# Routing of the last entry pair at the end of attention: one entry moved between the halves of the other's output projection, the rest alternated with early expert tiles

## The chip, the cores and the metric

The kernel runs on one NeuronCore of a Trainium2 chip. The metric is the device time of one execution in microseconds (us). Engines are named as in the profile: PE (TensorE matmuls), PEld (its weight loads), DVE (VectorE), ACT (ScalarE), POOL (GpSimd) and SP (SyncE, which here only issues DMAs).

## What is computed

All data are float32. An input of 2 x 2048 tokens of width 256 passes through four residual blocks: a state-space block, an expert layer, an attention block, and the same expert layer once more.

```python
x = x + attn_a(layernorm(x), ...)     # state-space scan
x = x + ffn(layernorm(x), Wr, br, Wl1, bl1, Wl2, bl2, biases_N)
x = x + attn_b(layernorm(x), w_qkv, w_out, ln_w, ln_b)   # attention over the 2 entries
x = x + ffn(layernorm(x), Wr, br, Wl1, bl1, Wl2, bl2, biases_N)
```

In the expert layer a router scores 8 experts for each token, the best two are kept, and their normalised weights mix the two results; an expert is `(silu(x W1a + b1a) * (x W1b + b1b)) W2 + b2` with a hidden width of 512. The attention here mixes only the two batch entries of one position with each other, in 16 heads of 64.

## The kernel before

**Groups.** Tokens are worked in groups of 512: four groups in time, `s` = 0 to 3 (`NS` = 4), for each of two batch entries `i` = 0, 1. Below, (0,3) is the first entry of the last group and (1,3) the second.

**Attention.** For each `s`, the loop at the end runs `mix(s)` (L1431: value projections times attention weights into two tiles `o`), `outward(s)` (L1454: the output projection), and then half of the scores of the next `s`. `outward` runs over the two entries and, in each, over two halves of two token tiles; a half is 16 matmuls into `pao` (L1462, each shown as two records), an addition to the residual `x` on DVE (L1470), and `aside.step(2)` (L1471).

**Work at the side.** `aside` is a list of Python generators. `aside.step(n)` runs the first one on to its n-th next `yield`, going over to the next generator when one ends; `aside.rest()` runs all of them to the end. So each `step` writes a piece of other work into the program at that point. After each entry `outward` appends `prepared(i, s)`, which routes that entry, and for the last group also `entered()`, which writes the routed entry's rows into the expert table.

**Routing of one entry**, `prepare` (L309), has six yields: (1) the write of `x` to the output (L316, SP) and the layernorm statistics; (2) the inverse root on POOL (L244); (3) the normalised `xn` (L248, DVE) and its write to `xnd` in DRAM (L318, SP); (4) eight transposes `pt_g` (L257), two ACT copies, eight router matmuls `pr_g` (L330); (5) the choice of two experts on DVE (L338 to L357); (6) two prefix matmuls `pk_g` (L363, L364) and the places `at` (L391); then the weights `pay` (L396 to L410), with one exponential on ACT (L398).

**Entering** (L412) then issues eight indirect DMAs from POOL (L433), each of which writes 128 rows of 12 bytes into the table, with a yield after every second one.

**Early tiles.** An expert tile is 256 token slots of one expert. Nine of them (called tiles 0 to 8 here; `ge` in names) are planned before routing is complete and are worked inside attention by the generator `last.early`, held in `tiles`. One tile takes three steps. The first fetches the weights of the next tile (L668 and L670, 1 MB and 0.5 MB, and the biases L672, L674, all on SP) with its two gathers (L683, POOL), transposes its own rows (`pxs`, L709, copied by ACT at L713), and does two of four up-projection parts (`pab`, L722; SiLU on ACT at L730, product on DVE at L731). The second does the other two parts. The third is the down-projection (`pf`, L792), the result `y` on DVE (L805), and two indirect DMAs that add the rows to the output (L816, POOL). Weights, gathered rows and `y` have two buffers each: tile n+2 loads its first weights when tile n's up-projection is over, and its second weights when its down-projection is.

**The end of attention.** At `s` = 3 `aside.rest()` empties the side list and `tiles.step(4)` brings the early tiles to the end of tile 1's up-projection. Then come `mix(3)` and `outward(3)`. Before the change, four steps of (0,3)'s routing were taken by the two `aside.step(2)` of the second entry; all that was left, and the whole of (1,3), was taken by `aside.rest()`; `last.plan()` (L515) plans the remaining tiles from the counts of all tokens on DVE; and `tiles.rest()` writes the rest of the early tiles, from tile 1's down-projection to tile 8. After that `last.run()` works the remaining tiles.

**What sets the order.** The order on SP is that of the program text. On the other engines a list scheduler orders the instructions inside this part; each engine then runs its own list strictly in order. Dependences through DRAM are tracked by tensor: the write of a whole entry of `x` to the output (L316) and the adding DMAs of early tiles (L816) stand in program order to each other, while the adding DMAs among themselves are declared independent.

Of the kernel before, what the change touches and what calls it, by code (L numbers as in the profile page):

```python
# [19 lines left out]
NS = L // TG  # L20
# [26 lines left out]
def kernel(  # L47
# [35 lines left out]
    def bank(tag, name):  # L83
        return ps.tile([P, 512], F32, tag=tag, name=name)
# [140 lines left out]
    aside = Aside()  # L225
# [672 lines left out]
    with tc.tile_pool(name="ssm1", bufs=1) as s1, tc.tile_pool(name="ssm2", bufs=2) as s2:  # L898
# [295 lines left out]
        tiles = Aside()  # L1194
# [65 lines left out]
    with tc.tile_pool(name="att1", bufs=1) as a1, tc.tile_pool(name="att2", bufs=2) as a2:  # L1260
# [33 lines left out]
        def prepared(b, s):  # L1294
            routed.append((order.index((b, s)) + 1, (yield from last.prepare(b, s, "T"))))

        def entered():
            while routed:
                n, group = routed.pop(0)
                yield from last.enter(*group)  # L1300
                if n in EARLY:
                    last.plan_early(n, EARLY[n], group[2])
                    tiles.step()
# [151 lines left out]
        def outward(s):  # L1455
            o = mixing[s]
            for i in range(2):
                for t in range(0, GT, 2):
                    po = bank("C", f"pao_{s}{i}{t}")
                    for j in range(2):  # L1460
                        for c in range(NA):
                            nc.tensor.matmul(  # L1462
                                po[:, j * DM : (j + 1) * DM],
                                o[i][:, c, (t + j) * P : (t + j + 1) * P],
                                w_o_sb[:, c, :],
                                start=(c == 0),
                                stop=(c == NA - 1),
                            )
                    x = xg[i, s][:, t : t + 2, :]
                    nc.vector.tensor_tensor(x, po.rearrange("p (t d) -> p t d", t=2), x, ALU.add)  # L1470
                    aside.step(2)  # L1471
                aside.add(prepared(i, s))
                if s == NS - 1 or s == NS - 2 and i:
                    aside.add(entered())
            if s + 3 < NS:
                aside.add(front(s + 3))
# [5 lines left out]
        tiles = Aside()  # L1482
# [5 lines left out]
        for s in range(NS):  # L1488

            if s + 1 < NS:  # L1490
                while s + 1 not in inputs:
                    aside.step()
                aside.add(entered())
                scores(s + 1, range(0, GT // 2))
            else:
                aside.rest()
                tiles.step(4)
            mix(s)
            outward(s)
            if s + 1 < NS:  # L1500
                scores(s + 1, range(GT // 2, GT))
                weights(s + 1)
        aside.rest()
        last.plan()
        tiles.rest()

# [63 lines left out]
```

## Time and profile before

| what | value |
|---|---|
| median of 3 runs | 1734.07 us (1732.85 to 1741.57) |
| profiled execution | 1733.28 us, of which 1731.6 us span |
| PE busy | 1596.9 us, 92% of the span |
| DVE, ACT, POOL busy | 901.2, 674.1, 734.1 us |
| mean granted TensorE clock | 0.969 |
| end of the last output projection | 1330.7 us from the span's start |
| early tiles 2 and 3: down-projection over | 1358.7 and 1380.5 us |
| one early tile after that | 11.8 us |
| last early tile (8): down-projection over | 1441.1 us |

A row of the timeline has the start, the busy time, the engine, line and operation, the tile written and those read, how many instructions are merged, and in brackets how long the engine was idle before it and what ended that. All times are us from the start of the span. In the list of waits, a row names the waiting engine and line, what it waited for, the time in total, how often, and the longest. "Remote" there means that the semaphore that was waited for came at no event that the profile can name.

### The profile page before, as it was taken

What the parts mean: (1) busy time and instruction counts of PE and PEld (TensorE: products, weight loads), DVE (VectorE), ACT (ScalarE), POOL (GpSimd) and SP (SyncE); (2) the same over time, 40 slices, a digit from 0 to 9 for tenths busy, and PEclk for the clock granted to TensorE, in tenths of its full rate; (3) what the DMA queues carried; (4) which work ended last, traced back from release to release, by engine and by line L of the source; (5) the groups of instructions that cost most, each with busy time, mean ns of one, the idle gap of its engine ahead of it and who ended that gap; (6) DMA issues with size and microseconds to landing.
All of it is one profiled execution on the core that took longest, in us unless ns stands there. A gap on an engine that the chain in (4) does not pass through costs nothing.

```text
span 1731.6 us, 21826 instructions
## 1 busy us (share of the span) xinstructions
PE 1596.9 (92%) x6928; PEld 1182.5 (68%) x6928; DVE 901.2 (52%) x2481; ACT 674.1 (39%) x1348; POOL 734.1 (42%) x702
## 2 busy tenths in 40 slices
PE   6997888989989997999998999899999699999997
PEld 4565555766767775787885575465768588888886
DVE  6778888737557465222237648447554522222222
ACT  4886877856546542222332202001121222333332
POOL 3346456445536565444442003403241543545443
PEclk9998998999989998999999999999999899999999
DMA  4111211634435362789852312606463568888882
GB/s 154 44 69 36 86 62 44 217 99 134 120 65 173 89 176 80 205 255 313 221 114 79 81 42 63 86 14 135 140 124 105 126 184 246 223 230 223 229 212 45
DMA packets 174742, 231.27 MB, mean 134 GB/s; under 512 B 45920, under 2 KB 138080, under 8 KB 174368
## 3 DMA queue, kind: packets, MB, share of 16 engines
q1 hardware_dynamic: 143520, 193.42, 37.8%
q0 software_dynamic: 31104, 36.42, 11.7%
q8 instruction: 56, 0.92, 0.2%
q14 instruction: 62, 0.51, 0.1%
HBM read 192.72 MB, written 37.06 MB: 133 GB/s over the span
## 4 chain that ended last, share of the span: by engine, by line
PE 66%; DMA 11%; DVE 11%; POOL 4%; ACT 3%; issue 3%; another core or an unknown queue 1%; SPq 0%; DVEq 0%; POOLq 0%; ACTq 0%
PE pab_g L722 8%; PE pao L1462 6%; PE pab_fe L722 5%; PE pq L1368 5%; PE pab_f L722 4%; PE pf_g L792 4%; PE pab_ge L722 4%; PE pf_fe L792 3%; PE pvd L1442 3%; DVE xc L1047 3%; PE pk L1368 3%; PE pf_f L792 2%; DMA lb<-sums 2%; PE pi L1143 2%; PE pc L1030 2%
## 5 line engine op out<-in xcount | busy, mean ns | idle before, releaser
L722 PE MATMUL pab_fe<-xT_fe,w_fe 128*128 128x256 f32 x672 | 163.1, 399 | 25.0 <-DVE gT_fe L731 18.5
L722 PEld LDWEIGHTS pab_fe<-xT_fe,w_fe 128*128 128x128 f32 x672 | 132.4, 200 | 53.8 <-DVE gT_fe L731 23.2
L722 PE MATMUL pab_g<-xT_g,w_g 128*128 128x256 f32 x736 | 162.9, 379 | 0.0
L722 PEld LDWEIGHTS pab_g<-xT_g,w_g 128*128 128x128 f32 x736 | 139.4, 190 | 19.1 <-ACT xT_g L713 0.4
L816 POOL DMA_INDIRECT out_dram<-y_g,tab_g x51 | 80.3, 1574 | 141.4 <-DVE y_g L805 62.0
L1368 PE MATMUL pq<-w_qkv_sb,axT 128*128 128x512 f32 x256 | 117.4, 598 | 0.0
L1047 DVE SCALAR_TENSOR_TENSOR xc<-pre,conv_w_sb,xc 128x512 f32<-128x512 f32 x144 | 112.5, 791 | 6.2 <-ACT xc L1039 5.5
L1462 PE MATMUL pao<-w_o_sb,o 128*128 128x256 f32 x512 | 112.0, 380 | 1.3 <-DVE o L1450 1.2
L1462 PEld LDWEIGHTS pao<-w_o_sb,o 128*128 128x128 f32 x512 | 97.0, 190 | 18.1 <-issue 2.9
L731 DVE SCALAR_TENSOR_TENSOR gT_g<-pab_g,b_g,sa_g 128x256 f32<-128x256 f32 x92 | 44.5, 484 | 117.8 <-ACT sa_g L730 107.8
L730 ACT ACTIVATE sa_g<-pab_g,b_g 128x256 f32<-128x256 f32 x92 | 43.6, 474 | 154.4 <-PE pab_g L722 140.9
L433 POOL DMA_INDIRECT table_g<-pay_g,at_g x64 | 62.1, 970 | 88.4 <-DVE w_g L409 55.0
L1030 PE MATMUL pc<-xT,w_in_sb 128*128 128x512 f32 x192 | 94.8, 623 | 0.4 <-ACT xc L1039 0.4
L792 PE MATMUL pf_g<-w_g,gT_g 128*128 128x256 f32 x408 | 92.9, 379 | 0.0
L1084 ACT ACTIVATE lt<-lb,cum 128x128 f32<-128x128 f32 x256 | 82.8, 393 | 21.2 <-DMA lb<-sums 21.2
L731 DVE SCALAR_TENSOR_TENSOR gT_fe<-pab_fe,b_fe,sa_fe 128x256 f32<-128x256 f32 x84 | 39.7, 481 | 95.1 <-ACT sa_fe L730 87.3
L1368 PEld LDWEIGHTS pq<-w_qkv_sb,axT 128*128 128x128 f32 x256 | 48.8, 193 | 58.8 <-issue 57.2
L722 PE MATMUL pab_ge<-xT_ge,w_ge 128*128 128x256 f32 x288 | 68.6, 393 | 17.2 <-ACT xT_ge L713 12.1
L816 POOL DMA_INDIRECT resid<-y_fe,tab_fe x42 | 67.1, 1598 | 35.6 <-DVE y_fe L805 15.2
L792 PE MATMUL pf_fe<-w_fe,gT_fe 128*128 128x256 f32 x336 | 80.6, 394 | 1.4 <-DVE gT_fe L731 1.2
L792 PEld LDWEIGHTS pf_g<-w_g,gT_g 128*128 128x128 f32 x408 | 75.4, 190 | 9.3 <-DVE gT_g L731 0.2
L1383 ACT ACTIVATE kd<-pk 128x512 f32<-128x512 f32 x32 | 19.1, 597 | 158.3 <-PE pk L1368 88.1
(493 smaller groups left out, 3458.5 us busy)
## 6 DMA issues: line engine op xcount, KB each, us to landing
w_g<-in_wl_dram SPq DMA_DIRECT2D x28, 1024.0 KB
w_fe<-in_wl_dram SPq DMA_DIRECT2D x21, 1024.0 KB
lb<-sums SPq DMA_DIRECT2D x32, 512.0 KB
w_f<-in_wl_dram SPq DMA_DIRECT2D x16, 1024.0 KB
o<-prob SPq DMA_DIRECT2D x32, 512.0 KB
w_g<-in_wl_dram SPq DMA_DIRECT2D x28, 512.0 KB
w_fe<-in_wl_dram SPq DMA_DIRECT2D x21, 512.0 KB
w_ge<-in_wl_dram SPq DMA_DIRECT2D x9, 1024.0 KB
```

The costliest lines, as they stand in the source:

```text
L433: i = nc.gpsimd.indirect_dma_start(out=self.table, out_offset=bass.IndirectOffsetOnAxis(ap=at[:, t, c : c + 1], axis=0), in_=pay[:, t, c, ...
L722: nc.tensor.matmul(p[:, q * n : (q + 1) * n], t["w1"][:, k, c * P : (c + 1) * P], t["xT"][:, k, :], start=(k == 0), stop=(k == KD - 1),)
L730: nc.scalar.activation(sa[:, :n], p[:, 0:n], AF.Silu, bias=t["b1"][:, i : i + 1])
L731: nc.vector.scalar_tensor_tensor(t["gT"][:, i, :n], p[:, n : 2 * n], t["b1"][:, NHT + i : NHT + i + 1], sa[:, :n], ALU.add, ALU.mult)
L792: nc.tensor.matmul(pos[h][:, h * DM : (h + 1) * DM], t["gT"][:, j, h * P : (h + 1) * P], t["w2"][:, j, :], start=(j == 0), stop=(j == NHT ...
L816: j = nc.gpsimd.indirect_dma_start(out=self.acc if self.direct else self.acc[: self.seq[i][4] or NT + TT, :], out_offset=bass.IndirectOffs ...
L1030: nc.tensor.matmul(pc, w_in_sb[:, k, DI + c * P : DI + (c + 1) * P], xT[:, k, :], start=(k == 0), stop=(k == KD - 1),)
L1047: nc.vector.scalar_tensor_tensor(xc[:, c, :], pre[:, c, j : j + TG], conv_w_sb[:, c, j : j + 1], xc[:, c, :], ALU.mult, ALU.add,)
L1084: nc.scalar.activation(lt[:, i, :], lb[:, i, :], AF.Relu, bias=g["cum"][:, t, i : i + 1], scale=-1.0)
L1368: nc.tensor.matmul(p, src[:, k, t * P : (t + 1) * P], w_qkv_sb[:, k, j, half * TG : (half + 1) * TG], start=(k == 0), stop=(k == KD - 1),)
L1442: nc.tensor.matmul(pvd, w_qkv_sb[:, k, 2, c * P : (c + 1) * P], xd[:, k, :], start=(k == 0), stop=(k == KD - 1),)
L1462: nc.tensor.matmul(po[:, j * DM : (j + 1) * DM], o[i][:, c, (t + j) * P : (t + j + 1) * P], w_o_sb[:, c, :], start=(c == 0), stop=(c == NA ...
```

## The change

Two edits. In `outward`, for the last group, each half is followed by four steps of the side list in place of two. At entry 0 the list is empty, so this acts on entry 1 alone: (0,3) is now taken eight steps, four between the halves and four behind them, which is its whole routing and half of its entering. And `aside.rest()` at the end becomes a loop that alternates one step of the side list with one step of the early tiles. In the program this moves (0,3)'s transposes and router matmuls on PE ahead of the last half of `pao`, and the early tiles' steps, with their weight loads on SP and their gathers and adding DMAs on POOL, in among the steps of (1,3). Nothing is added or removed.

```diff
                     x = xg[i, s][:, t : t + 2, :]
                     nc.vector.tensor_tensor(x, po.rearrange("p (t d) -> p t d", t=2), x, ALU.add)
-                    aside.step(2)
+
+                    aside.step(4 if s == NS - 1 else 2)
                 aside.add(prepared(i, s))
                 if s == NS - 1 or s == NS - 2 and i:
                     aside.add(entered())
...
             if s + 1 < NS:
                 scores(s + 1, range(GT // 2, GT))
                 weights(s + 1)
-        aside.rest()
+        while aside.waiting:
+            aside.step()
+            tiles.step()
         last.plan()
         tiles.rest()
```

The orders that result, as the two built programs have them (tile numbers as above):

| engine | before | after |
|---|---|---|
| PE | last half of pao; pt (0,3); pr (0,3) among pf of tile 1; pxs 2; pk (0,3), pt, pr and pk (1,3) among pab 2; pf 2; pxs 3 | pt (0,3); last half of pao with pr (0,3) in it; pk (0,3); pf 1; pxs 2; pt (1,3) and pab 2; pf 2; pxs 3; pr (1,3); half of pab 3; pk (1,3); rest of pab 3; pf 3 |
| POOL | half of gather 4; adds of tile 1; half of gather 4; 8 + 8 table writes; gather 5 and adds of tile 2 | half of gather 4; 6 table writes; adds of tile 1; 2 table writes; half of gather 4; gather 5 and adds of tile 2; 8 table writes |
| SP | x, xn (0,3); x, xn (1,3); weights 3; weights 4 | x, xn (0,3); weights 3; x, xn (1,3); weights 4 |

On SP, the write of x (1,3) waited in the program before only for its data and its queue; in the changed program it also waits for the two adds of tile 1, and the adds of tile 2 on POOL wait for it.

## The prediction

> **What bounds the kernel now.** I read the page's slices first: PE is busy in nine tenths or more of almost every slice, and the change touches the one late hole, slice 32 of 40 (1342 to 1385 us).
>
> ```profile
> PE   6997888989989997999998999899999699999997
> ```
>
> From 1450 to 1700 us PE is without a gap, so what is saved in the hole comes off the end. The timeline of PE there:
>
> ```profile
> 1346.46 1.56 PE L722 MATMUL pab_ge<-xT_ge,w_ge 128*128 128x256 f32 x6 [0.78 <-DVE gT_ge L731]
> ...
> 1349.82 1.99 PE L722 MATMUL pab_ge<-xT_ge,w_ge 128*128 128x256 f32 x8 [0.92 <-issue]
> ...
> 1356.41 2.43 PE L792 MATMUL pf_ge<-w_ge,gT_ge 128*128 128x256 f32 x10 [3.13 <-DVE cump_g L548]
> 1358.67 0.60 PE L709 MATMUL pxs_ge<-ident,xs_ge 128*128 128x128 f32 x4
> 1367.77 9.41 PE L722 MATMUL pab_ge<-xT_ge,w_ge 128*128 128x256 f32 x32 [8.51 <-ACT xT_ge L713]
> 1377.02 3.67 PE L792 MATMUL pf_ge<-w_ge,gT_ge 128*128 128x256 f32 x16
> ```
>
> The idle times in brackets, with one of 0.92 at 1338.40, sum to 14.3 us, and tile 3's 32 records take 9.41 us where tile 4's take 7.17. What is late? The last gap waits for ACT's copy of transposes that PE shows as over at 1359.3. The list of waits from 1335 to 1370:
>
> ```profile
> ACT xT_ge L713 <- remote: 12.4, 1, 12.4
> ...
> ACT sa_ge L730 <- remote: 4.9, 1, 4.9
> ```
>
> ACT waits 8 us after the work it needs; SP's second weights and POOL's next gather wait for PE's semaphore as well, and small DVE operations of the plan wait 1 to 2 us for one another. The semaphores lag on every engine. What runs meanwhile is on POOL:
>
> ```profile
> 1344.25 0.99 POOL L433 DMA_INDIRECT table_g<-pay_g,at_g  x1 [0.30 <-issue]
> ...
> 1363.23 0.95 POOL L433 DMA_INDIRECT table_g<-pay_g,at_g  x1 [0.30 <-issue]
> 1367.37 0.99 POOL L683 DMA_INDIRECT xs_ge<-xnd_g,tab_ge  x1 [3.19 <-remote]
> ```
>
> Sixteen table writes of 128 rows of 12 bytes, one each 1.26 us; the lag begins some 5 us into them and ends 3 us behind them. It is no accident of this place: semaphore events lag by up to 7.7 and 8.6 us in the sixteens from 1107 and from 1249, and at 667 to 690, where six writes, a pause of 7 us and eight writes stand in the first expert layer, PE shows
>
> ```profile
> 687.89 0.60 PE L709 MATMUL pxs_fe<-ident,xs_fe 128*128 128x128 f32 x4
> 692.03 8.86 PE L722 MATMUL pab_fe<-xT_fe,w_fe 128*128 128x256 f32 x32 [3.54 <-issue]
> ```
>
> nothing at the six, then 3.54 us idle at the eight. That the writes cause the lag is inferred from their standing together.
>
> **The change, part by part.** No instruction is added or taken out.
>
> *(0,3) between the halves.* The last half of pao is 32 records of 0.219 us, 7.0 us. Before it PE now does eight transposes (0.87 us) and in it the router matmuls (1.7 us), which until now stood behind it; pao ends at 1330.7 + 0.87 + 1.7 = 1333.3. On PE that is a trade at nothing: xn (0,3) is ready at 1321.6 (its DVE row ends then), the transposes come at 1323.7, and the pao matmul between covers ACT's copies of 0.6 us each; without that cover it would be 0.6 us. (1,3)'s residual is 2.6 us later. DVE then does (0,3)'s places among (1,3)'s statistics, and of pay's last steps one stands behind tile 1's second y, so pay is ready at about 1339.9, against 1342.2 before.
>
> *(1,3) and the early tiles.* PE: pk to 1333.8, tile 1's pf (3.5) to 1337.3, pxs 2 (0.45) to 1337.8. Then come six of eight transposes of (1,3), whose xn waits for statistics, POOL's power (1.04) and three DVE passes of 0.41: 1338.9, so PE waits about 1 us. Tile 2's pab 7.0 and the rest of the transposes: 1346.9; pf 2 to 1350.4; pxs 3, pr (1,3) 1.7: 1352.6; half of pab 3: 1356.1. There pk waits for DVE's choice, and tile 3's first SiLU stands on ACT behind (1,3)'s exponential and two table loads of 1.28 us; the product behind pk on DVE feeds the next PSUM bank. I take 1.5 us (ends: 0.8, the like gap at 1346.46, and 3). PE is at 1358, with pab 3 at 1361.5, with pf 3 at 1365.0. Before, tile 3's pf ends at 1380.5; from there a tile takes 11.8 us on both sides. Lead without any lag: 15.5 us.
>
> *The table writes.* They are no longer sixteen in a row: six from 1339.9, two adds of tile 1, two more to about 1354, then gathers and tile 2's adds, then (1,3)'s eight from about 1361 or a little later. What the lag costs then, no row shows for this order. Lower end: nothing, as at the six from 667. Upper end: the old price, 14.3 + 2.2. A pair of eights from 1183 and 1200 shows lags of 3.3 and 7.5 us (there PE had other work). I take the row at 692, for it is nearest: six, a break, eight, with an early tile's chain to be fed. Its price is 3.54 + (8.86 - 7.17) = 5.2 us; with 1 us for the first eight, 6.2.
>
> [...] I keep 6.2, since the row's 3.54 us gap did pay 1.69.
>
> *SP.* Tile 3's weights now go ahead of x and xn of (1,3). Their second half must wait for pf 1 (1337.3), as before (1338.4): free. But x (1,3) now waits for tile 1's adds, which POOL issues behind six table writes: 1339.9 + 6 x 1.26 = 1347.5, the second at 1349.4. [...] The trace's landing events of such adds are 3.6 to 4.6 us when DMA is calm and 6.6 under load; I take 5: 1354.4. Behind it on SP stand xn (1,3) and tile 4's weights, issued 1.8 us later, 1356.2; these landed 5.3 us after issue with one 0.5 MB write ahead of them, now there are two (1.4 more): 1363. [...] Xn (1,3) itself is read only by gathers of the last stage, about 1410. Tile 2's adds wait for x (1,3) on POOL to about 1358, and gather 5's second half behind them has until 1377. The plan on DVE ends before 1380, and SP needs it at about 1403.
>
> Sum: 15.5 - 6.2 = 9.3 us off the profiled execution's 1733.3: 1724.0. The median of the runs is 0.8 us above that execution: 1725.
>
> **Rivals.** *The pair of eights sets the price.* Lags of 3.3 and 7.5 us, less about 1 us of slack each, and 2.2 for the clock: 11, gain 4.5, 1730. For it: eight writes follow eight after about 8 us here too. Against: scatters and gathers stand between.
> *No lag at all*: eights are short enough. Gain 15.5, 1718.5. For it the six at 667; against it every eight in the trace.
> *The change doesn't do what it says*: the eights lag as the sixteen did, and the gap only moves. 15.5 - 14.3 - 0.5: 1733.
> *Slower.* The wait of x (1,3) on SP for tile 1's adds holds up tile 4's weights. Every us that the adds land after 1358 is a us of PE at tile 4; the lead is used up at 1358 + 9 = 1367, and half a per cent is lost at 1376, 27 us after issue. The longest landing of an indirect DMA in this part is 10 us, behind a queue of broadcasts, so it needs the writes of the table to dam the queue far more than they now do. 1744 then.
>
> **How the numbers follow.** A measurement of this kernel can tell about 0.5% from no change: 8.7 us, so faster means below 1725.4. Nearest row 45% (1725, half of it on either side of that bound), pair of eights 25% (1730), no lag 15% (1718.5), gap only moved 8% (1733), slower 7% (1744). Faster: 0.24 + 0.15 and a part of the spread of the pair, 0.46; slower 0.07; the rest 0.47. The range 1716 to 1733 takes in the first four but for their edges: the unknown costs are the lag (0 to 15 us) and the wait at pk (0.8 to 3).
>
> **What would show it.** Right: pao ends near 1333; tile 3's pf ends 8 to 14 us before 1380.5; the table writes stand as 6, 2 and 8; PE's gaps at tiles 2 and 3 are 1 to 2 us, with one of 3 to 5 at tile 4 or 5, by the end of the last eight, and a granted clock under 1 behind it. Wrong: gaps of over 5 us near 1350 or 1372; a wait of tile 4's pab for w_ge; gather 5 or 6 as what ends a PE gap; or tile 3 early but the last stage starting late, so that the lead is lost behind tile 8.

## The result, and the profile after

The changed kernel takes 1727.33 us, the median of 20 runs (1719.77 to 1738.76); the kernel before, run beside it, 1734.6 us (1728.1 to 1743.5, 20 runs). The ratio is 0.9962 with a 95% interval of 0.9948 to 0.9977, that is 6.6 us less (4.0 to 9.0). Forecast were 9.3 us less and 1725.0. The profiled execution of the changed kernel has a span of 1726.6 us, 5.0 less than that of before.

PE in the 40 slices of the page, after the change:

```profile
PE   6997888989989996999998999899999799999997
```

Slice 32 (1338 to 1381 us) is now at 7 in place of 6. The hole is shallower, but it is there. PE's timeline through it:

```profile
1324.52 6.29 PE L1462 MATMUL pao<-w_o_sb,o 128*128 128x256 f32 x28
...
1356.13 5.27 PE L722 MATMUL pab_ge<-xT_ge,w_ge 128*128 128x256 f32 x16 [1.39 <-DVE gT_ge L731]
1361.23 3.67 PE L792 MATMUL pf_ge<-w_ge,gT_ge 128*128 128x256 f32 x16
1364.74 0.60 PE L709 MATMUL pxs_ge<-ident,xs_ge 128*128 128x128 f32 x4
1367.83 3.72 PE L722 MATMUL pab_ge<-xT_ge,w_ge 128*128 128x256 f32 x16 [2.49 <-issue]
1377.50 6.51 PE L722 MATMUL pab_ge<-xT_ge,w_ge 128*128 128x256 f32 x16 [5.95 <-DVE gT_ge L731]
1383.85 3.67 PE L792 MATMUL pf_ge<-w_ge,gT_ge 128*128 128x256 f32 x16
1387.36 0.60 PE L709 MATMUL pxs_ge<-ident,xs_ge 128*128 128x128 f32 x4
```

Tile 3's down-projection is over at 1364.7, where the kernel before has 1380.5. But the one long gap has become one of 5.95 us in tile 4, with a slow clock behind it (granted 0.56; 16 records in 6.51 us where 3.72 is usual). Tile 4 ends at 1387.4 against 1392.3, and from there both kernels take 11.8 us a tile. On POOL, the table writes stand as forecast, six, two and eight. Shown are the last of the six, the adds behind them, and the first and last of the eight:

```profile
1343.42 0.97 POOL L433 DMA_INDIRECT table_g<-pay_g,at_g  x1 [0.30 <-issue]
1344.69 1.62 POOL L816 DMA_INDIRECT out_dram<-y_ge,tab_ge  x1 [0.30 <-issue]
...
1356.34 1.62 POOL L816 DMA_INDIRECT out_dram<-y_ge,tab_ge  x1 [3.01 <-DVE gT_ge L731]
...
1361.48 0.99 POOL L433 DMA_INDIRECT table_g<-pay_g,at_g  x1 [0.30 <-DVE cump_g L548]
...
1370.38 0.95 POOL L433 DMA_INDIRECT table_g<-pay_g,at_g  x1 [0.30 <-issue]
```

The 3.01 us before 1356.34 I read as tile 2's adds waiting for x (1,3): their y is ready at 1348.9, and SP issues x at 1350.7. The gap in tile 4 begins about 1 us behind the issue of the last of the eight writes and ends 7 us behind it.

**A measure that can be compared.** The last output projection does not end at the same time in every execution, although all before it is in the same order: equivalently 1328.2 us here and 1330.9 in the execution before. So I use distances from the end of the last `pao`, with 2.6 us added where the router work of (0,3) stands ahead of it. "To tile 3" is to the first transposes behind tile 3's down-projection, "to tile 4" likewise, "to tile 8" is to the start of its down-projection.

| execution | to tile 3 | to tile 4 | to tile 8 |
|---|---|---|---|
| before | 49.7 | 61.5 | 106.8 |
| after | 36.5 | 59.1 | 104.3 |

The lead of 13.2 us at tile 3 is 2.4 at tile 4. The other 2.6 us of the difference between the spans arose ahead of this stage, where PE runs the same instructions in the same order in both kernels. That is the spread between executions: in the fourteen traces of this document the output projection ends, on this measure, between 1328.2 and 1343.7 us, on chips of either kind.

### The profile page after: what moved, and what is told of

Its sections match the earlier page's. It is cut to its first block, busy times and chain, and to the rows that moved or that the text cites. A ratio compares the mean times of both kernels' runs of the same rounds, so it can differ in the third digit from the quotient of the medians.

```text
span 1726.6 us, 21824 instructions
## 1 busy us (share of the span) xinstructions
PE 1595.6 (92%) x6928; PEld 1182.0 (68%) x6928; DVE 900.0 (52%) x2481; ACT 673.9 (39%) x1348; POOL 734.6 (43%) x702
## 3 DMA queue, kind: packets, MB, share of 16 engines
q0 software_dynamic: 31104, 36.42, 11.8%
## 4 chain that ended last, share of the span: by engine, by line
PE 66%; DVE 11%; DMA 10%; POOL 5%; issue 3%; ACT 3%; SPq 1%; DVEq 0%; POOLq 0%; ACTq 0%
PE pab_g L722 8%; PE pao L1462 6%; PE pq L1368 5%; PE pab_fe L722 5%; PE pab_f L722 4%; PE pf_g L792 4%; PE pab_ge L722 3%; PE pvd L1442 3%; PE pf_fe L792 3%; DVE xc L1047 3%; PE pk L1368 3%; PE pf_f L792 2%; PE pi L1143 2%; DMA lb<-sums 2%; DMA out_dram<-y_g,tab_g 2%
## 5 line engine op out<-in xcount | busy, mean ns | idle before, releaser
L722 PE MATMUL pab_ge<-xT_ge,w_ge 128*128 128x256 f32 x288 | 70.0, 401 | 16.1 <-DVE gT_ge L731 10.6
```

Of the source, the lines that this page charges most:

```text
L722: nc.tensor.matmul(p[:, q * n : (q + 1) * n], t["w1"][:, k, c * P : (c + 1) * P], t["xT"][:, k, :], start=(k == 0), stop=(k == KD - 1),)
```

## The experiments

State of the theories at the start: mine was that early tiles fill the hole, and that lag of the semaphores behind the table writes limits it. Rivals: the first edit alone is the gain; the lag comes from something else.

**Each edit alone, and the changed kernel without writes.** Four kernels on one chip. The first keeps `aside.step(4 ...)` and has `aside.rest()` back; the second keeps the loop and has `aside.step(2)` back. The other two replace the entering, from (1,3) on or from (0,3) on (`n >= 8` or `n >= 7`). They leave the rows of these entries out of the table; routing, plan and tiles stay. The cut shows the case `n >= 8`:

```diff
-                yield from last.enter(*group)
+                if n >= 8:
+                    for _ in range(GT):
+                        yield
+                else:
+                    yield from last.enter(*group)
```

> First edit alone: four side steps behind each half of the last group, then the side list is emptied as before. POOL then has eight writes of (0,3), tile 1's adds, both halves of gather 4, eight writes of (1,3), and the early tiles stay where they stood. Theory (the gain is tile 3's early place in the hole, and what is left of the hole is semaphore lag behind the table writes): only the splitting of the sixteen writes helps, -1 to -4 us against the kernel before, with the idle times of PE before tile 3 still over 6 us in sum and tile 3's down-projection still over 44 us behind the end of the last output projection. Rival (the gain comes from routing (0,3) between the halves): -6 to -7 us, as the whole change gave.

> Second edit alone: two side steps behind each half as before, then side list and early tiles alternate. POOL then has tile 1's adds, eight writes of (0,3), gather 5 with tile 2's adds, gather 6 with tile 3's adds, eight writes of (1,3). Theory: nearly the whole gain, -4 to -8 us against the kernel before, with tile 3's down-projection over 36 to 41 us behind the end of the last output projection and a gap of several us, with a slow clock behind it, within 8 us of the end of the last eight writes, now one tile later than in the changed kernel. Rival (routing between the halves is the gain): within 1.5 us of the kernel before.

> The changed kernel without the eight table writes of (1,3): that entry's rows are left out of the expert table (its routing, the plan and all tiles stay). Theory (the table writes make the semaphores lag): the gap of 6 us in tile 4's up-projection and the slow clock behind it go, tiles 4 and later come 8 to 10 us earlier relative to the end of the output projection; -12 to -17 us against the kernel before. Rival (the lag comes from the weight loads or the plan on DVE): the gap stays, -6 to -7 us as the changed kernel. Rival (SP's wait of x (1,3) for tile 1's adds): no change either, since that wait stays.

> The changed kernel without the sixteen table writes of (0,3) and (1,3): the rows of both entries are left out of the table. Theory: as without (1,3)'s eight, and 0 to 3 us more, since the first eight cost PE about 1 us idle and 1.5 us of clock at tile 3: -13 to -19 us against the kernel before, no PE gap over 1.5 us after the output projection but the one for the first transposes. Rival (weight loads or the plan): -6 to -7 us, gap and slow clock stay.

| kernel | median us | ratio to before (95%) | to tile 3 | to tile 4 | to tile 8 |
|---|---|---|---|---|---|
| before, same chip | 1725.26 | | | | |
| first edit alone | 1727.94 | 1.0018 (0.9997 to 1.004) | 36.7 | 48.5 | 94.2 |
| second edit alone | 1725.86 | 0.9996 (0.9969 to 1.0023) | 31.7 | 46.0 | 91.9 |
| no writes of (1,3) | 1723.95 | 0.9992 (0.9967 to 1.0017) | 34.1 | 46.4 | 91.8 |
| no writes of both | 1723.39 | 0.9985 (0.9963 to 1.0007) | 34.2 | 46.3 | 91.6 |

My four expectations fail, and the rivals' with them, except that the second edit alone is within 1.5 us, as the rival to it said; but the first edit, from which that rival had the gain, gives none either. Nothing is gained, not even without the writes, and the kernel before is itself 9 us faster here. Nor is there any lag in the traces: the kernel with the first edit alone issues sixteen writes (eight, a pause of 7 us, eight), and its tiles run at 11.8 us at once. The traces differ in one more thing. They hold 2202 to 2207 semaphore events of DVE, counted in the records of each trace; those of before and after hold 2017 and 1985. Either the chip makes the lag, or the orders of writes that these kernels have avoid it.

**The two kernels again.** So both went to the chip unchanged.

> The kernel before, unchanged, profiled again, since the four runs so far met no lag at all, with sixteen, eight or no table writes, and the kernel before had a median of 1725.3 us beside them and 1734.6 us beside the changed one. Theory A (the lag is not caused by the table writes; it belongs to the chip or the hour of the first measurement): if this call's runs of the kernel before lie near 1725 us, its idle times after the output projection sum to 3 to 5 us, not 14.3, and tile 3's down-projection is over 34 to 37 us behind the last output projection, not 49.8. Theory B (the sixteen writes in a row cause it, and the first edit alone and the second alone each break them up): the gap of about 8 us before tile 3 is there again, 49 us.

> The changed kernel, unchanged, on the same chip as the run of the kernel before. Theory A: where the kernel before lies near 1725 us, within 2.5 us of it, and no gap of 6 us in tile 4; where it lies near 1734 us with its gap, -5 to -8 us. Theory B: -5 to -8 us in either case, with tile 4's gap.

This was another chip. The kernel before took 1745.09 us there (23 runs; 1745.86 as a run of its own, ratio 0.9998, 0.9981 to 1.0015), the changed one 1742.60: ratio 0.9976 (0.9957 to 0.9994), 4.2 us less, a little under the 5 to 8 us that both theories named. The lag is there (2013 and 1997 events), and so is the hole. PE in the kernel before on this chip:

```profile
1371.20 4.63 PE L792 MATMUL pf_ge<-w_ge,gT_ge 128*128 128x256 f32 x10 [5.08 <-issue]
1375.63 1.06 PE L709 MATMUL pxs_ge<-ident,xs_ge 128*128 128x128 f32 x4
1380.90 10.12 PE L722 MATMUL pab_ge<-xT_ge,w_ge 128*128 128x256 f32 x32 [4.21 <-issue]
```

And in the changed kernel, from the end of tile 3 to the end of tile 4:

```profile
1382.63 0.60 PE L709 MATMUL pxs_ge<-ident,xs_ge 128*128 128x128 f32 x4
1389.44 9.60 PE L722 MATMUL pab_ge<-xT_ge,w_ge 128*128 128x256 f32 x32 [6.22 <-issue]
1398.88 3.68 PE L792 MATMUL pf_ge<-w_ge,gT_ge 128*128 128x256 f32 x16
1402.39 0.60 PE L709 MATMUL pxs_ge<-ident,xs_ge 128*128 128x128 f32 x4
```

Distances: 50.7, 62.5 and 107.8 us before; 40.1, 59.9 and 105.1 after. Again a lead of over 10 us at tile 3 and of 2.6 at tile 4. On a chip with the lag, then, what the first profiles showed repeats.

**The kernel before without its sixteen writes, and the last writes in pairs.** The first is the edit above with `n >= 7` in the kernel before. The second is a candidate for a better order: the last entering is alternated with three tile steps in place of one, and its writes are held behind the adds of the tile ahead (the cut below, against the changed kernel).

```diff
                 apart(j, f"add_{nm}", "tokens differ")
+                if tag == "B" and self.direct:
+                    pool(j)
...
-            tiles.step()
+            tiles.step(1 if len(aside.waiting) > 1 or routed else 3)
```

> The kernel before without the sixteen table writes of (0,3) and (1,3): the rows of both entries are left out of the table. Theory B' (on a chip where the semaphores lag, the table writes bring it on): if the kernel before's median here is over 1732 us, its idle times between the last output projection and tile 3's end fall from 12 to 14 us to 3 to 5, tile 3's down-projection is over 34 to 38 us behind the output projection, not 50, and the time is 10 to 16 us less. Theory A' (the lag of such a chip stands at this place for another reason: the plan, the weight loads, the copies of x): over 46 us, and within 3 us of the kernel before. On a chip without the lag (median near 1725 us): within 3 us by both, and nothing is told apart.

> The changed kernel with (1,3)'s eight table writes spread: two behind the adds of each of tiles 3 to 6, held there on POOL, instead of eight in a row behind tile 2's adds. Theory B': on a chip with the lag the gap of 6 us and the slow clock at tile 4 go, since two writes in a row are not enough, -8 to -13 us against the kernel before. Theory A': -2 to -7 us as the changed kernel, the gap stays at tile 4. On a chip without the lag: within 3 us of the kernel before, unless the last pair now holds up the first table load of the last stage, which would cost 1 to 5 us.

The chip was one without the lag (2205 and 2202 events, the kernel before 1725.27 us). Without writes: 1724.51 us, ratio 1.0001 (0.998 to 1.0021), distances 36.4, 48.2 and 93.5. In pairs (6 runs): 1734.35 us, ratio 1.0055 (1.0034 to 1.0077), slower by 9.5 us, where I had allowed 1 to 5. PE at tile 8 in that kernel:

```profile
1411.90 0.60 PE L709 MATMUL pxs_ge<-ident,xs_ge 128*128 128x128 f32 x4
1418.68 0.47 PE L709 MATMUL pxs_g<-ident,xs_g 128*128 128x128 f32 x1 [6.17 <-DMA xs_g<-xnd_g,tab_g]
1423.49 1.50 PE L709 MATMUL pxs_g<-ident,xs_g 128*128 128x128 f32 x4 [4.34 <-DMA xs_g<-xnd_g,tab_g]
1426.65 0.48 PE L709 MATMUL pxs_g<-ident,xs_g 128*128 128x128 f32 x1 [1.66 <-DMA xs_g<-xnd_g,tab_g]
1426.92 9.18 PE L722 MATMUL pab_ge<-xT_ge,w_ge 128*128 128x256 f32 x32
```

The last pair is issued at 1408.6 and 1409.9; the tables of the last stage must wait for it, its gathers for the tables (POOL issues the first at 1415.8), and PE for the gathers, 12.2 us in three gaps, and tile 8's up-projection behind them takes 9.18 us where 7.08 is usual, 2.1 us more. Whether pairs avoid the lag was not seen, for lack of lag.

**The changed kernel on a chip without the lag**, and the kernel without writes once more.

> The changed kernel, unchanged, once more, because it has not yet stood beside the kernel before on a chip without the lag. Theory C (the change gains only where the semaphores lag; elsewhere both kernels fill the place after the output projection about equally): on a chip whose semaphore records are whole and where the kernel before lies near 1725 us, within 3 us of it, with gaps of PE of about 1 us each and tile 3's down-projection over 34 to 36 us behind the last output projection; on a chip with the lag, -4 to -7 us. Rival (the gain is of the order itself): -6 to -7 us on both.

> The kernel before without the sixteen table writes of (0,3) and (1,3), a second time, for a chip with the lag (the rows of both entries are left out of the table). If it meets one: by the theory that the table writes bring the lag on, -10 to -16 us against the kernel before and tile 3's down-projection over 34 to 38 us behind the output projection; by the theory that the lag stands there for another reason, within 3 us and over 46. On a chip without the lag: within 3 us, as the first time.

Again a chip without lag (2207 and 2205 events; the kernel before 1725.79 us). The changed kernel: 1728.70 us, ratio 0.9997 (0.9972 to 1.0022). The medians lie 2.9 us apart, inside that interval (4.8 us less to 3.8 more), which leaves out the 6 to 7 us less of the rival. So theory C holds: without the lag no gain is seen. PE, from the end of the output projection to the end of tile 4:

```profile
1339.48 6.29 PE L1462 MATMUL pao<-w_o_sb,o 128*128 128x256 f32 x28
...
1370.26 3.72 PE L722 MATMUL pab_ge<-xT_ge,w_ge 128*128 128x256 f32 x16 [1.25 <-DVE gT_ge L731]
...
1377.36 0.60 PE L709 MATMUL pxs_ge<-ident,xs_ge 128*128 128x128 f32 x4
1378.93 7.14 PE L722 MATMUL pab_ge<-xT_ge,w_ge 128*128 128x256 f32 x32 [0.98 <-ACT xT_ge L713]
...
1389.42 0.60 PE L709 MATMUL pxs_ge<-ident,xs_ge 128*128 128x128 f32 x4
```

Its distances are 34.2, 46.2 and 96.3. Without writes: 1725.78 us, 0.9997 (0.9977 to 1.0017); 36.4, 48.2 and 93.4. No trace of the kernel before with its writes was taken on a chip without the lag; the kernel without them stands for it, since their times agree.

So even here the changed kernel is 2.0 us ahead of that one at tile 4 and 2.9 behind at tile 8. What takes it back is seen on POOL and then on PE, in the changed kernel's trace of this chip:

```profile
1386.06 0.96 POOL L433 DMA_INDIRECT table_g<-pay_g,at_g  x1 [0.30 <-issue]
1387.32 0.99 POOL L683 DMA_INDIRECT xs_ge<-xnd_g,tab_ge  x1 [0.30 <-issue]
1388.62 1.61 POOL L816 DMA_INDIRECT out_dram<-y_ge,tab_ge  x1 [0.30 <-issue]
...
1417.02 1.59 POOL L816 DMA_INDIRECT out_dram<-y_ge,tab_ge  x1 [3.55 <-DMA out_dram<-y_ge,tab_ge]
1418.92 1.57 POOL L816 DMA_INDIRECT out_dram<-y_ge,tab_ge  x1 [0.31 <-DMA tab_g<-table_g]
1420.79 1.02 POOL L683 DMA_INDIRECT xs_g<-xnd_g,tab_g  x1 [0.30 <-issue]
```

```profile
1427.73 0.87 PE L709 MATMUL pxs_g<-ident,xs_g 128*128 128x128 f32 x4 [2.21 <-DMA xs_g<-xnd_g,tab_g]
1430.11 0.48 PE L709 MATMUL pxs_g<-ident,xs_g 128*128 128x128 f32 x1 [1.51 <-DMA xs_g<-xnd_g,tab_g]
1430.38 9.29 PE L722 MATMUL pab_ge<-xT_ge,w_ge 128*128 128x256 f32 x32
```

Tile 3's rows are ready at 1378.8, but POOL is in (1,3)'s eight writes and issues the adds at 1388.6. From there each tile's adds are late, and two pairs of them wait for the landing of the pair ahead, 2.79 us at 1408.6 and 3.55 us at 1417.0; the first gathers of the last stage come behind them, and PE waits 3.7 us for these (2.21 and 1.51), and the up-projection behind them takes 2.2 us more (9.29 in place of 7.08). In the kernels without (1,3)'s writes the lead of 1.8 us is still there at tile 8 (91.8 and 91.6 against 93.5). That the eight writes set off this row of delays is read from this one trace and those two.

**Do table writes bring on the lag, where there is lag?** Once more the kernel without writes, which met the fourth chip without lag; and then, as the last kernel, eight writes more in the kernel before, at a place where nothing of the kind stands. They go into a spare table, so nothing is left out; further lines, not shown, make that table and hold the writes behind tile 4's adds on POOL.

```diff
+                if i == 5 and self.direct:
+                    pay, at = self.kept
+                    for q in range(2 * GT):
+                        with tc.issue_after(on_pool[0]):
+                            w = nc.gpsimd.indirect_dma_start(
+                                out=self.spare,
+                                out_offset=bass.IndirectOffsetOnAxis(ap=at[:, q // 2, q % 2 : q % 2 + 1], axis=0),
+                                in_=pay[:, q // 2, q % 2, :],
+                                in_offset=None,
+                            )
                 self.turn(i)
```

> The kernel before without the sixteen table writes of (0,3) and (1,3), for a chip with the lag, which the two runs so far did not meet (the rows of both entries are left out of the table). If the kernel before lies over 1732 us here and the semaphore records are incomplete: -10 to -16 us and tile 3's down-projection over 34 to 38 us behind the output projection by the theory that the table writes bring the lag on; within 3 us and over 46 by the theory that it stands there for another reason. If it lies near 1725 us: within 3 us, and the cause of the lag stays open.

> The kernel before with eight more writes of the same kind (128 rows of 12 bytes, into a spare table that nobody reads), on POOL between tile 4's adds and the gather behind them, where PE runs its steady 11.8 us a tile. The part before them is the kernel before itself. On a chip without the lag (the kernel before near 1725 us, whole semaphore records): tile 3's down-projection is over 35 to 37 us behind the last output projection, the sixteen writes stand in a row all the same, and the eight more cost nothing: within 3 us. On a chip with the lag, if table writes bring it on: a PE gap of 3 to 7 us with a slow clock within 12 us of the eight, at tile 5 or 6, and +4 to +9 us; if the lag at the end of attention has another cause: the tiles keep 11.8 us, within 3 us. On either chip POOL has 10 us more to do at one tile, which the two buffers of gathered rows should cover; if they don't, tile 6's transposes wait for a gather by name.

The first: 1727.06 us, 0.9997 (0.9977 to 1.0016) of the kernel before (1727.19), distances 36.4, 48.2 and 93.6; it tells nothing new. The second met a chip with the lag (2009 events; the kernel before 1744.03 us): 1745.95 us, ratio 1.0014 (0.9993 to 1.0034). POOL and PE at the added writes (the lines of this kernel are shifted by two and more):

```profile
1403.21 0.99 POOL L849 DMA_INDIRECT spare_g<-pay_g,at_g  x1 [0.30 <-issue]
...
1412.10 0.96 POOL L849 DMA_INDIRECT spare_g<-pay_g,at_g  x1 [0.30 <-issue]
```

```profile
1405.53 3.67 PE L794 MATMUL pf_ge<-w_ge,gT_ge 128*128 128x256 f32 x16
1409.04 0.60 PE L711 MATMUL pxs_ge<-ident,xs_ge 128*128 128x128 f32 x4
1410.32 5.83 PE L724 MATMUL pab_ge<-xT_ge,w_ge 128*128 128x256 f32 x24 [0.67 <-ACT xT_ge L715]
1418.46 3.66 PE L724 MATMUL pab_ge<-xT_ge,w_ge 128*128 128x256 f32 x8 [2.32 <-issue]
1421.96 3.67 PE L794 MATMUL pf_ge<-w_ge,gT_ge 128*128 128x256 f32 x16
```

From tile 5's down-projection to tile 6's it is 16.4 us in place of 11.8. The waits from 1400 to 1422 name no weight and no gather:

```profile
DVE gT_ge L733 <- ACT sa_ge L732: 10.9, 6, 3.5
ACT sa_ge L732 <- issue: 5.8, 4, 2.0
ACT sa_ge L732 <- PE pab_ge L724: 5.1, 2, 3.8
DVE gT_ge L733 <- issue: 3.8, 1, 3.8
ACT xT_ge L715 <- issue: 3.5, 1, 3.5
```

DVE and ACT wait up to 3.8 us for one another and for nothing, as at the end of attention. No entry is routed and no plan is made here, and weights come as at every tile; only the writes are new, and the two gathers and two adds of each tile, also indirect, stand at the tiles before and behind as well, where a tile takes 11.8 us. So on this chip, one with the lag, eight table writes were enough to bring it on: 4.6 us in this trace, of which 2.3 are idle and 1.8 slower records (8 in 3.66 us in place of 1.9). The idle time is less than the 3 to 7 us that I had expected, and the time of 1.9 us more (1.2 less to 5.9 more) falls short of the 4 to 9 us and does not exclude zero. Ahead of the added writes the kernel before shows its usual distances, 49.9 and 61.7.

**The same eight writes in all fourteen traces.** A row that no edit touches tells the two kinds of chip apart: the eight writes in the first expert layer, to which the prediction's price goes back. Here the changed kernel at its next tile, first with the lag, then on the chip without:

```profile
690.66 8.66 PE L722 MATMUL pab_fe<-xT_fe,w_fe 128*128 128x256 f32 x32 [4.05 <-issue]
694.89 7.17 PE L722 MATMUL pab_fe<-xT_fe,w_fe 128*128 128x256 f32 x32 [0.68 <-ACT xT_fe L713]
```

In the five traces with incomplete events PE is idle for 2.33 to 4.05 us there, in the nine with all events for 0.67 or 0.68, though the writes and their order are the same. So it is not the orders of writes that avoid the lag. What was not done: no kernel without the sixteen writes met a chip with the lag, so that the hole at the end of attention goes with them is not shown; and the writes were added in one trace only.

## Why the prediction was right, and where not

**The hole and its cause.** Right for a chip with the lag, as far as was seen: one trace with writes added brings on a gap, and none with writes taken out met such a chip. Wrong as a statement about the kernel: in four of the seven sets of runs, each on a chip of its own, the kernel before takes 1725 to 1727 us, and the sixteen writes cost nothing there (1.0001, 0.9997 and 0.9997 without them). A forecast from one profiled execution could not know this.

**(0,3) between the halves: a trade at nothing.** Agrees: the first edit alone gives 1.0018 (0.9997 to 1.004), and its distances to tiles 3 and 4 are those of the kernel before without writes, to 0.3 us. In the changed kernel PE waited 0.24 us for xn (1,3) where I took 1, and 1.8 (0.43 and 1.39) at pk and the product behind it where I took 1.5.

**The lead without any lag, 15.5 us.** Right: the changed kernel without lag has 34.2 us to tile 3, the kernel before with lag 49.7.

**The price of the lag: here the prediction failed.** The step that failed is the 6.2 us for the lag, taken from the row at 692. To tile 4, the changed kernel has 59.1 and 59.9 us with the lag and 46.2 without it. The price is 12.9 and 13.7 us, about twice what I took: 2.3 and 5.9 by tile 3, 10.6 and 7.8 at tile 4. Before the change it is 13.3 (61.5 less 48.2). So two parts, of eight and eight, cost what sixteen in a row cost, and in the profiles the change gives 2.4 to 2.7 us of the 9.3: my rival that the gap only moves, a little better than I priced it. The row itself I had read rightly; in the other traces with the lag it costs much the same (idle time and clock together 3.4 to 5.7 us). What did not hold is that one such row stands for this place. Here an eight follows the six and two after 11 to 12 us, with adds and gathers between, and both parts cost. Why they cost more than the eight at 692 or the added eight (4.6 us) is not shown.

**That the number came out close** is in good part luck. The stage gives 2.5 us in the first pair of profiles and 2.7 in the second; the rest of those pairs' differences (2.6 and 1.2) lies in work that both kernels do alike. The timed gains, 6.6 (4.0 to 9.0) and 4.2 (1.0 to 7.5), are larger than what the stage shows; for the first, 2.5 us lies below the interval. So the profiles account for less than half of the first gain. Whether the lag costs the kernel before more in other executions than in the profiled ones, or whether the rest is drift, stays open.

**SP.** Right: x (1,3) waited for tile 1's adds, tile 2's adds waited 3.01 us for x, and no weight was late. The adds landed 4.0 to 4.6 us after issue where I took 5. By that 5, tile 4's weights land at 1363, 3.5 us ahead of its up-projection at 1366.5; 1354.4 and these 3.5 us make the 1358 of the slower rival. In the trace the up-projection starts at 1367.83, and no engine waits for a weight there. What I listed last among the things that could go wrong, that the lead is lost at the last stage, happens on the chip without the lag, through POOL rather than SP.

**Gaps and the clock behind them.** I kept 6.2 us because the row's gap of 3.54 us was followed by 1.69 us of slower records. What follows a gap differs from place to place. In the kernel before, the 3.13 us at 1356.41 were followed by full speed (granted clock 1.00, 10 records in 2.43 us), the 8.51 us at 1367.77 by a granted clock of 0.75 (32 in 9.41 in place of 7.17). In the changed kernel the 2.49 us at 1367.83 were followed by full speed as well (1.00, 16 in 3.72), the 5.95 us at 1377.50 by 0.56 (16 in 6.51), and two gaps of only 0.43 and 1.39 us in tile 3 by 0.69 (16 in 5.27 in place of 3.72). The 2.32 us at the added writes were followed by 8 records in 3.66 us in place of 1.9 (granted clock 0.90 from 1405.5 to 1421.9, and 1.00 in the 11.8 us before and behind). So in these traces the length of one gap does not tell whether a slow clock follows. What decides was not found.

## What to carry to other kernels

Before you rearrange a kernel to fill a hole, ask whether the hole is a dependence or a lag: where engines wait for work that the trace shows as done, profile the same kernel on a second chip, because the hole may not be there: here the kernel before took 1734 to 1745 us in three sets of runs and 1725 to 1727 in four. Work moved into such a hole need not make the lag smaller; here it met the lag one tile later (5.95 us in tile 4). And look at what stands behind small scatters before you spread them: in pairs they made this kernel 9.5 us slower, since the last of them stood ahead of what reads the table (PE waited 12.2 us), and in the changed kernel on the chip without the lag the eight stood ahead of tile 3's adds on POOL, which were ready at 1378.8 and issued at 1388.6.

## What the runs showed of the hardware

- The chips differed. In three of the seven sets of runs the kernel before took 1734 to 1745 us. The traces of these show engines that start several us behind work that is over (8 us in the kernel before: ACT's copy starts at 1367.13, PE's transposes for it are over at 1359.3), during and after rows of eight or more indirect writes of 128 rows of 12 bytes, and they lack about a tenth of DVE's semaphore events (1985 to 2017 of some 2205). In the other four it took 1725 to 1727 us, with all events and no lag. At the eight writes of the first expert layer PE is idle for 2.33 to 4.05 us in the five traces of the first kind and for 0.67 or 0.68 in the nine of the second. What makes a chip, or its hour, the one or the other was not found. All runs were recorded. Whether the lag is there without recording, or has to do with the events that are missing, was not tried either.
- In the changed kernel with the lag the granted clock was 0.83 from 1356 to 1386 us; on the chip without it, it was 1.00 from 1356 to 1386 us, and the two up-projections that follow tile 3 there take the usual 7.14 and 7.17 us. So in this trace the lag cost PE twice, by the gap (5.95 us in tile 4) and by the slow clock behind it (16 records in 6.51 us in place of 3.72).
- Executions of one kernel on one chip spread over 8 to 19 us (1718.4 to 1736.6 for the kernel before on one of them). Half a per cent, 8.6 us, lies inside that spread, so a single run of each kernel can't tell it.
